# Attention's first scores among the last outputs of the feed-forward in front of it, and new orders for some first tiles

## The chip, the cores and the metric

The kernel runs on one core of one Trainium2 chip. The metric is the device time of one execution, in microseconds (us); of several runs the median counts. The engines are TensorE (PE; its weight loads, PEld, overlap its matmuls), VectorE (DVE), ScalarE (ACT), GpSimd (POOL) and SyncE (SP), which mostly issues DMAs. PE's clock is granted by a throttle; the profile shows it as a share of full speed.

## What is computed

Two layers, each with attention and a feed-forward part, and each part added to its input after a normalisation:

```python
x = L0_attn_x                                    # [2, 1024, 512] float32
x = x + _layernorm(_L0_attn_ref(_layernorm(x), Wq, bq, Wkv, bkv))
x = x + _layernorm(_L0_ffn_ref(_layernorm(x), w1, w2, w3))     # h = 1408
x = x + _layernorm(_L1_attn_ref(_layernorm(x), q_w, kv_w, c_w))
x = x + _layernorm(_L1_ffn_ref(_layernorm(x), w_gate, w_up, w_down))
```

The first attention is one within a token (32 heads of 16, four groups): no token sees another. The first feed-forward rounds its weights to −1, 0 and 1 by their mean size (`clip(round(w / mean|w|))`) and computes `sigmoid(x w1') * (x w2')`, times w3'. The second attention is causal over 1024 tokens, with 16 query heads and 4 key heads of 32, rotary positions on q and k, and a softmax of `q k' / sqrt(32)`. The second feed-forward keeps the two largest of every four hidden values. All of it is float32.

## The kernel before

The 2048 tokens are 16 tiles of 128 (x_sb, resident in SBUF). Four tiles make a group of 512 columns (GT = 4), and there are four groups (NG = 4) and two batches of eight tiles (TB = 8). One function holds everything. PE's and POOL's instructions stand in the order of the program (`manual_schedule`, L612 and L1021); those of DVE, ACT and SP are ordered by a scheduler, except for DVE in the first statistics (L613). Each engine then runs its instructions in that order, each waiting for its semaphores. Tiles come from pools, in which a tag with `bufs` buffers is used in turn, so a new tile waits for the last use of the one it replaces. Pools opened on the right side and on the left are stacks; a pool that is closed gives its room to those opened later, whose tiles wait for the uses of what lay there.

**First attention (L222 to 300).** Per tile: l0_stats (statistics, a root on ACT), l0_pre (L235: normalise on DVE, four transposes on PE into a psum bank, copy by ACT), l0_post (L243: pq and pkv, four matmuls each and one with `ones_r` and `bias` that adds the bias, L249). The bias is loaded by four small DMAs on SP's queue (L155, L156) into `braw`, behind the first four tiles of x; POOL splits it in two parts (L157 to 160: bhi, then bias). Beside it the weights of the feed-forward are loaded into large buffers (big, L129: tag raw, two buffers, used in turn by raw1, raw2, raw3 and by xTg_0 to xTg_3) and rounded: quant_sums on ACT (L312), a sum over partitions on PE (psum_w, L322) and a threshold (quant_limits, L321), quant_apply on DVE (L331).

**First feed-forward (L365 to 411, L682 to 753).** Per group g and hidden chunk hc (HC = 11): l0_hidden issues 16 ph matmuls (L371, two banks of ps_a), a sigmoid on ACT (L376), the product h on DVE (L377), and splits h into two parts hl on ACT and POOL (L379, L380). l0_out (L385) follows some chunks later (outs, L678): 8 po matmuls of a chunk into four banks. At the group's last chunk, po is normalised and added to x_sb (ln_stats with ACT's sqrt, L177; tmp on DVE, for group 3 in turn on ACT, L405; add on POOL, L411). During a group the next group's transposed input is made (l0_xT_stats, l0_xT_norm, l0_xT). In g = 2 at hc 4 the first pool p0 is closed and the pool aw opened in its room, and attention's weights are loaded there. In g = 2 at hc 5 and 9, a1_stats (L504) makes the statistics of batch 0's tiles 0 to 3 and 4 to 7; its root is made by small DVE operations (inverse_root, L182).

**Second attention, projections (project_parts, L522).** A tile's projection has three parts. First: normalise into xn (two buffers, tag xn, shared with rope's rbq and with tmp of the last norm), four transposes pxt, copy xT. Second: pq (L556) and pkv (L561), rope on DVE (ra L579, rbk and rbq L584), adds on POOL (L588). Third: transposes pkT and pqT, split into hl, two DMAs to a DRAM tile dq (L608). Batch 0's tiles 0 to 3 are projected during group 3; parts of tiles 4 to 6 stand after its last ph (L691 to 694), followed by all outputs still pending (L697, L753: four po groups, 32 matmuls).

**Second attention, tasks.** A task is a batch, a group Q of 512 queries and one key head g with its four query heads; there are 16. A task needs q (load_q, L803) and k (load_k, L809; three buffers) read back from dq on SP's queue, four DMAs each; their tiles are in pool s1, opened after the feed-forward's pools are closed (L754 to 759). score_step (L815): the product psc with the mask added by a second matmul (L824, L830), the negated maximum on DVE (mxs, L835), the exponential with its sum on ACT (L839, result thrown away in a junk tile). shifts and minus_log (L845, L873; small DVE operations) turn maxima and sums into one shift per row, which PE transposes (pmt, L795). prob_step (L893): pst (L900, L907), exponential pT (L913), for the diagonal a select on POOL (L915). value_step (L922): po (L929). Later output_parts (L939). Between them run batch 1's projections and pieces of the last feed-forward's weights (POOL, with DMAs on POOL's queue, L465). The lead-in, L1065 to 1083, is hand-written: loads of tasks 0 and 1, the remaining parts of tiles 4 to 7, the scores of task 0, then of task 1:

```python
load_upto(2)
parts[GT][2]()
...
parts[GT + 2][1]()
parts[GT + 1][2]()
...
parts[GT + 3][0]()
scores_up_to(1, -2)
parts[GT + 3][1]()
parts[GT + 2][2]()
...
```

The last feed-forward (from L1180) is not touched; its first weights are loaded when f1_begin (L1106) closes aw.

Of the kernel before, what the change touches and what calls it, by code (L numbers as in the profile page):

```python
# [24 lines left out]
def two_layer_sandwich(  # L25
# [76 lines left out]
    ones = keep.tile([P, P], F32, tag="ones", name="ones")  # L102
    nc.gpsimd.memset(ones, 1.0)
# [9 lines left out]
    aw_stack, l0_stack, p0_stack = ExitStack(), ExitStack(), ExitStack()  # L113
    p0 = p0_stack.enter_context(tc.tile_pool(name="p0", bufs=1, side="right"))
    w0 = l0_stack.enter_context(tc.tile_pool(name="w0", bufs=1))
# [12 lines left out]

    def big(name, dtype):  # L129
        return s0.tile([P, DC * H0], dtype, tag="raw", name=name)  # L130
# [23 lines left out]
    for row in (0, 32):  # L154
        nc.sync.dma_start(out=braw[row : row + 1, :D], in_=a0_bq.unsqueeze(0))  # L155
        nc.sync.dma_start(out=braw[row : row + 1, D:], in_=a0_bkv.unsqueeze(0))  # L156
# [10 lines left out]
    def ln_stats(pool, srcs, name, roots=True):  # L167

        n = len(srcs)
        st = pool.tile([P, n, 6], F32, tag=f"st{n}", name=f"st_{name}")  # L170
# [214 lines left out]
    def l0_out(g, hc, hl):  # L385
# [8 lines left out]
        if hc == HC - 1:  # L394
# [4 lines left out]
            mv, rs = ln_stats(pool, po, f"f0o_{g}")  # L399
# [104 lines left out]
    def a1_stats(st, G):  # L504
        tiles = [x_sb[:, st.b * TB + G * GT + k, :] for k in range(GT)]
        mv, rs = ln_stats(aw, tiles, f"a1_{st.b}_{G}", roots=False)
        st.ln[G] = mv, rs, minus_mean(aw, mv, rs, GT)
# [103 lines left out]

    with tc.manual_schedule(engines={mybir.EngineType.PE, mybir.EngineType.Pool}):  # L612
        with tc.manual_schedule(engines={mybir.EngineType.DVE}):  # L613
# [6 lines left out]
        th1 = quant_limits(part1, "w1", ps_o("psum_w1"))  # L620
        l0_pre(2)
        l0_post(1)
        l0_stats(1)
# [58 lines left out]
        for g in range(NG):  # L682
            nxt = None
            for hc in range(HC):
                pend.append((g, hc, l0_hidden(g, hc, xs.T)))
# [3 lines left out]
                if g == NG - 1 and hc == HC - 1:  # L689

                    parts[GT][1]()  # L691
                    parts[GT + 1][0]()
                    parts[GT + 1][1]()
                    parts[GT + 2][0]()

                if hc == HC - 1:
                    outs(2)  # L697
                elif hc != 2 and (g > 0 or hc > 2):
                    outs(1)
# [14 lines left out]
                else:  # L714
# [10 lines left out]
                    elif hc == 2 * GT + 1:  # L725
                        parts[GT - 1][2]()
                        done[0] = GT
                        parts[GT][0]()
                step = HC * g + hc
# [5 lines left out]
                if g == NG - 2 and hc == 4:  # L735
# [13 lines left out]
                    nc.sync.dma_start(out=sinq_t, in_=ropeq_sin.rearrange("(t p) f -> p t f", p=P))  # L749
                if g == NG - 2 and hc in (5, 9):  # L750
                    a1_stats(batch(0), hc // 9)
            xs = nxt
        outs(len(pend))  # L753
# [9 lines left out]
    identb = wc_pool.tile([P, P], BF16, tag="identb", name="identb")  # L763
    nc.vector.tensor_copy(identb, ident)
    cmaskb = wc_pool.tile([P, P], BF16, tag="cmaskb", name="cmaskb")
    cmask = s1.tile([P, D], F32, tag="xn", name="cmask", bufs=1)[:, :P]
    make_causal_mask(nc, cmask, mask_val=-3.0e38)
    nc.vector.tensor_copy(cmaskb, cmask)
# [31 lines left out]

    def load_q(tk):  # L803
        tk.q = s1.tile([P, REP, GW], F32, tag="q4", name=f"q4_{tk.nm}", bufs=4)
        src = tk.st.d[tk.Q][:, :, tk.g, :].rearrange("s (r d) t -> s d r t", r=REP)
        for blk in range(4):
            nc.sync.dma_start(out=tk.q[blk * DK : (blk + 1) * DK], in_=src[blk % 2])

    def load_k(st, G):  # L809
        st.k[G] = s1.tile([P, NKV, GW], F32, tag="k4", name=f"k4_{st.b}_{G}", bufs=3)  # L810
        src = st.d[G][:, :, NKV, :].rearrange("s (g d) t -> s d g t", g=NKV)
        for blk in range(4):
            nc.sync.dma_start(out=st.k[G][blk * DK : (blk + 1) * DK], in_=src[blk // 2])
# [775 lines left out]
```

## Time and profile before

| what | value |
|---|---|
| three runs | 1544.43, 1539.05, 1537.12 us |
| median | 1539.05 us |
| profiled execution | 1543.98 us |
| its span | 1542.3 us |
| granted PE clock, mean | 0.97 |
| busy: PE, DVE, ACT, POOL | 95%, 66%, 47%, 20% |
| mean DMA rate | 109 GB/s |

The profile is of one execution, and times in it are us from the start of its span. A share of busy time is a mean over stages that are bound by different things; what a change of one stage is worth is read in that stage. The chain of waits follows the work that ended last in a window back to what released it. The windows give busy times in a stretch, with the granted clock. In a timeline, brackets give an engine's idle time in front of an instruction, and what ended it.

### The profile page before, as it was taken

To read this page: it belongs to the slowest core of one execution; us is meant where nothing else is said; L and a number is where in the kernel's file an instruction comes from. 1 tells how busy PE (TensorE), PEld (TensorE's weight loads), DVE (VectorE), ACT (ScalarE), POOL (GpSimd) and SP (SyncE) were. 2 spreads that over 40 slices of the span, in tenths; PEclk is the share of its full clock that TensorE was granted. 3 is DMA by queue.
4 is the path that set the end of the run, shared out by engine and by line. 5 is a ranking of instruction groups with operands and counts; after the bars stand their busy time and mean duration, and the time that the engine had idled before them with its cause. 6 is when DMAs were issued, how large, how long until landed. Compare 5 with 4: busy or idle time off the path is not lost.

```text
span 1542.3 us, 20375 instructions
## 1 busy us (share of the span) xinstructions
PE 1466.8 (95%) x6998; PEld 1052.4 (68%) x6998; DVE 1012.8 (66%) x2408; ACT 728.6 (47%) x1849; POOL 315.8 (20%) x420
## 2 busy tenths in 40 slices
PE   7999999899779999999899999999999999999997
PEld 3558888777445544544444446888888888888886
DVE  6976456542567777656768645786578468846783
ACT  4243343232268765797686983451245034404430
POOL 1105475232302323322332002000100010001001
PEclk9999999999869999999889999999999999999998
DMA  7201211201563343243342002643353345235411
GB/s 293 75 14 41 69 55 49 48 18 52 114 159 94 94 122 98 92 133 95 96 110 109 2 1 89 246 144 143 130 210 118 143 171 191 96 143 201 161 48 75
DMA packets 78751, 167.52 MB, mean 109 GB/s; under 512 B 10100, under 2 KB 35702, under 8 KB 76600
## 3 DMA queue, kind: packets, MB, share of 16 engines
q1 hardware_dynamic: 72936, 148.40, 29.9%
q0 software_dynamic: 4656, 16.52, 2.9%
q10 hardware_dynamic: 1056, 1.31, 0.3%
q8 instruction: 55, 0.90, 0.2%
q14 instruction: 48, 0.39, 0.1%
HBM read 138.94 MB, written 27.26 MB: 108 GB/s over the span
## 4 chain that ended last, share of the span: by engine, by line
PE 75%; DVE 10%; ACT 8%; issue 3%; POOL 2%; DMA 2%; SPq 0%; ACTq 0%; DVEq 0%; POOLq 0%
PE acc L1349 12%; PE pb_u L1198 7%; PE pb_g L1198 7%; PE ph L371 7%; ACT junk L839 5%; PE po L390 4%; PE pc_g L1198 4%; PE pc_u L1198 4%; PE psc L824 4%; PE pq L248 3%; PE py L945 3%; PE pq L556 3%; PE pst L900 3%; PE po L929 3%; DVE mxs L835 3%
## 5 line engine op out<-in xcount | busy, mean ns | idle before, releaser
L835 DVE TENSOR_REDUCE mxs<-psc 128x1 f32<-128x512 f32 (+3 forms) x384 | 195.7, 551 | 83.0 <-PE psc L824 43.0
L839 ACT ACTIVATE junk<-psc,mxs 128x512 bf16<-128x512 f32 (+3 forms) x384 | 221.7, 626 | 34.1 <-DVE mxs L835 28.7
L913 ACT ACTIVATE pT<-pst 128x512 f32<-128x512 f32 (+3 forms) x384 | 159.5, 547 | 89.8 <-PE pst L907 89.4
L371 PE MATMUL ph<-xTg,w 128*128 128x512 f32 x704 | 169.9, 394 | 4.9 <-DVE h L377 2.4
L824 PE MATMUL psc<-k,q 128*128 128x512 f32 (+3 forms) x384 | 146.2, 456 | 15.6 <-ACT junk L839 8.0
L371 PEld LDWEIGHTS ph<-xTg,w 128*128 128x128 f32 x704 | 131.5, 188 | 33.6 <-DVE h L377 3.3
L900 PE MATMUL pst<-q,k 128*128 128x512 f32 (+3 forms) x384 | 123.4, 413 | 16.2 <-ACT junk L839 12.0
L824 PEld LDWEIGHTS psc<-k,q 128*128 128x128 f32 x384 | 77.9, 215 | 79.8 <-ACT pT L913 30.0
L1402 POOL TENSOR_TENSOR x_sb<-x_sb,o 128x512 f32<-128x512 f32 x14 | 19.1, 1362 | 549.2 <-DVE o L199 549.1
L1349 PE MATMUL acc<-wd,h 128*128 128x256 f32 x512 | 121.6, 379 | 0.0
L900 PEld LDWEIGHTS pst<-q,k 128*128 128x128 f32 x384 | 68.3, 197 | 61.6 <-ACT junk L839 35.1
L915 POOL TENSOR_SCALAR_AFFINE_SELECT pT<-pT 128x256 f32<-128x256 f32 x128 | 51.9, 413 | 271.2 <-ACT pT L913 268.8
L1349 PEld LDWEIGHTS acc<-wd,h 128*128 128x128 f32 x512 | 97.2, 190 | 12.9
L839 ACT ACTIVATION_READ_ACCUMULATOR junk<-psc,mxs 128x1 f32 x384 | 96.1, 251 | 0.0
L929 PE MATMUL po<-pT,v 128*32 128x512 f32 (+3 forms) x768 | 94.1, 529 | 1.3 <-POOL pT L915 0.9
L1349 PE MATMUL acc<-wd,hx 128*128 128x256 f32 x384 | 93.3, 379 | 0.0
L380 POOL TENSOR_TENSOR hl<-h,hl 128x512 fp32r<-128x512 f32 x44 | 56.9, 1297 | 162.4 <-ACT hl L379 162.3
L390 PE MATMUL po<-w,hl 128*128 128x512 f32 x352 | 87.7, 394 | 0.6 <-DVE tmp L199 0.6
L377 DVE TENSOR_TENSOR h<-h,ph 128x512 f32<-128x512 f32 x44 | 30.0, 683 | 88.3 <-PE ph L371 78.5
L1349 PEld LDWEIGHTS acc<-wd,hx 128*128 128x128 f32 x384 | 73.1, 190 | 9.8
L1259 DVE TENSOR_TENSOR gate<-gate,ab 128x1024 f32<-128x1024 f32 x32 | 39.2, 1225 | 58.9 <-ACT ab L1256 58.9
L390 PEld LDWEIGHTS po<-w,hl 128*128 128x128 f32 x352 | 66.8, 190 | 15.3 <-DVE tmp L199 1.4
(268 smaller groups left out, 2825.6 us busy)
## 6 DMA issues: line engine op xcount, KB each, us to landing
w<-kept SPq DMA_DIRECT2D x64, 512.0 KB, 5.7
q<-dq SPq DMA_DIRECT2D x64, 256.0 KB, 5.2
wd<-keptd SPq DMA_DIRECT2D x16, 1024.0 KB, 7.9
w<-in_f_wg SPq DMA_DIRECT2D x32, 384.0 KB, 3.4
w<-in_f_wu SPq DMA_DIRECT2D x32, 384.0 KB, 5.4
wd<-in_f_wd SPq DMA_DIRECT2D x16, 768.0 KB, 5.8
dq<-hl SPq DMA_DIRECT2D x32, 320.0 KB, 3.2
kept<-wl POOLq DMA_DIRECT2D x16, 512.0 KB, 3.0
```

The costliest lines, as they stand in the source:

```text
L371: nc.tensor.matmul(pa, wt[:, c, cols], xT[:, s, c, :], start=(c == 0 and s == 0), stop=(c == DC - 1 and s == 1),)
L380: nc.gpsimd.tensor_tensor(hl[:, 1, :], h, hl[:, 0, :].bitcast(F32), ALU.subtract)
L390: nc.tensor.matmul(pos0[g][k], hl[:, s, k * P : (k + 1) * P], w3[:, hc, :], start=(hc == 0 and s == 0), stop=(hc == HC - 1 and s == 1),)
L824: nc.tensor.matmul(pa[:, :w], tk.q.bitcast(F32R)[:, r, ii * P : (ii + 1) * P], st.k[ch].bitcast(F32R)[:, g, :w], start=True, stop=True,)
L835: nc.vector.tensor_reduce(mx, pa[:, :w], AX.X, ALU.max, negate=True)
L839: nc.scalar.activation(junk[:, :w], pa[:, :w], AF.Exp, bias=mx, accum_out=tk.sm[:, ii, r, ch : ch + 1])
L900: nc.tensor.matmul(pas[r][:, c0:], st.k[j // GT].bitcast(F32R)[:, g, (j % GT) * P : (j % GT + 1) * P], tk.q.bitcast(F32R)[:, r, c0:], star ...
L913: nc.scalar.activation(p[:, e, c0:], pas[2 * pr + e][:, c0:], AF.Exp)
L915: nc.gpsimd.affine_select(out=p[:, :, c0 : c0 + P], in_=p[:, :, c0 : c0 + P], compare_op=ALU.is_ge, fill=0.0, base=0, pattern=[[0, 2], [1, ...
L929: nc.tensor.matmul(tk.po[DK * r : DK * r + DK, c0:], st.v[j // GT][:, j % GT, g * DK : (g + 1) * DK], tk.pT[j, r // 2][:, r % 2, c0:], sta ...
L1198: nc.tensor.matmul(p, a[:, c, :], b[:, c, :], start=(first and c == 0), stop=(c == 1), skip_group_check=not first,)
L1349: nc.tensor.matmul(acc[m // 2][:, m % 2 * HW : (m % 2 + 1) * HW], a[:, j, k * P : (k + 1) * P], b[:, j, :], start=start, stop=True, skip_g ...
```

## The change

It has these parts.

- The four bias loads are issued on POOL's queue in place of SP's. ACT is put in program order too in the first statistics. l0_pre(2) and l0_post(1) come ahead of the first threshold (th1).
- big takes its buffers in turn from s0 (one buffer) and from a new pool rb (one buffer), which is closed in f1_begin. An eighth large tile, "qk", reuses the buffer of xTg_2; at g = 3, hc = 9, behind the third part of tile 3, task 0's k and q are loaded into it.
- Task 0's 16 scores stand after the last ph, in halves of two heads between the po groups of the last chunks, the second part of tiles 4 and 5 and the first of tiles 5 and 6. Their psum banks are from ps_a, their junk tiles from s0 (tag h).
- The last norm of the feed-forward takes its root on DVE (inverse_root) in place of ACT's sqrt.
- In g = 2 from hc = 4 on, DVE is in program order. identb and the mask are made there. a1_stats of batch 1's first half is called at g = 3, hc = 4; that of its second half takes a tile that the logarithms also use (lgp).
- k4 has two buffers. The small tiles of minus_log have one shape (small_tile). In the lead-in task 0's shifts come first, and task 1's scores stand, one step each, between parts of tiles 4 to 7. From the first pmt on, PE's order is that of before.

Cut to its core:

```diff
 def big(name, dtype):
-    return s0.tile([P, DC * H0], dtype, tag="raw", name=name)
+    n_big[0] += 1
+    if n_big[0] % 2:
+        return s0.tile([P, DC * H0], dtype, tag="raw", name=name, bufs=1)
+    return rb.tile([P, DC * H0], dtype, tag="raw", name=name)
...
 for row in (0, 32):
-    nc.sync.dma_start(out=braw[row : row + 1, :D], in_=a0_bq.unsqueeze(0))
-    nc.sync.dma_start(out=braw[row : row + 1, D:], in_=a0_bkv.unsqueeze(0))
+    nc.gpsimd.dma_start(out=braw[row : row + 1, :D], in_=a0_bq.unsqueeze(0))
+    nc.gpsimd.dma_start(out=braw[row : row + 1, D:], in_=a0_bkv.unsqueeze(0))
...
-            mv, rs = ln_stats(pool, po, f"f0o_{g}")
+            mv, rs = ln_stats(pool, po, f"f0o_{g}", roots=not last)
...
 def a1_stats(st, G):
+    late = st.b == B - 1 and G == NQ - 1
+    mv, rs = ln_stats(
+        aw, tiles, f"a1_{st.b}_{G}", roots=False, st=small_tile("lgp", "st_late") if late else None
+    )
...
-    with tc.manual_schedule(engines={mybir.EngineType.DVE}):
+    with tc.manual_schedule(engines={mybir.EngineType.DVE, mybir.EngineType.Activation}):
...
-    th1 = quant_limits(part1, "w1", ps_o("psum_w1"))
     l0_pre(2)
     l0_post(1)
+    th1 = quant_limits(part1, "w1", ps_o("psum_w1"))
...
 for hc in range(HC):
+    order = ExitStack()
+    if g == NG - 2 and hc > 3:
+        order.enter_context(tc.manual_schedule(engines={mybir.EngineType.DVE}))
...
     if g == NG - 1 and hc == HC - 1:
-        parts[GT][1]()
-        parts[GT + 1][0]()
-        parts[GT + 1][1]()
-        parts[GT + 2][0]()
+        tk = tasks[0]
+        score_sums(tk, aw)
+        halves = [
+            lambda ii=ii, r=r: score_step(
+                tk, tk.q, tk.st.k[0], ii, 0, range(r, r + 2), ps_a, waste0
+            )
+            for ii in range(GT) for r in (0, 2)
+        ]
+        out1 = lambda: outs(min(1, len(pend)))
+        for f, n in (
+            (parts[GT][1], 0), (out1, 1), (parts[GT + 1][0], 1), (out1, 1),
+            (parts[GT + 1][1], 2), (out1, 1), (parts[GT + 2][0], 1), (out1, 1),
+        ):
+            f()
+            for h in halves[:n]:
+                h()
+            del halves[:n]
...
     elif hc == 2 * GT + 1:
         parts[GT - 1][2]()
         done[0] = GT
         parts[GT][0]()
+        tk = tasks[0]
+        tk.st = batch(0)
+        both = big("qk", F32)[:, : 2 * NKV * GW].rearrange(
+            "p (n r t) -> p n r t", n=2, r=REP
+        )
+        tk.st.k[0], tk.q = both[:, 0], both[:, 1]
+        fill_k(tk.st.k[0], tk.st, 0)
+        fill_q(tk.q, tk)
...
+    if g == NG - 1 and hc == 4:
+        a1_stats(batch(1), 0)
...
-        outs(len(pend))
...
 load_upto(2)
+scored(tasks[0])
 parts[GT][2]()
 finish(0, GT)
 parts[GT + 2][1]()
 parts[GT + 1][2]()
 finish(0, GT + 1)
 bank[0] = ring
+scores_up_to(pos + 1, -1)
 parts[GT + 3][0]()
-scores_up_to(1, -2)
+scores_up_to(pos + 1, -1)
 parts[GT + 3][1]()
+scores_up_to(pos + 1, -1)
 parts[GT + 2][2]()
 finish(0, GT + 2)
-scores_up_to(2, -2)
+scores_up_to(pos + 1, -1)
 parts[GT + 3][2]()
 finish(0, GT + 3)
-scores_up_to(s_end[0], -2)
 scores_up_to(wanted(-1), -1)
```

fill_k and fill_q issue the DMAs of load_k and load_q; score_step takes the q and k tiles, the maker of banks and the maker of junk tiles as arguments; scored(task) calls shifts and puts maxima_T on the list of what is due.

## The prediction

> **What bounds the kernel now.** I read the page's slices first, for the places where TensorE (PE) is not full; then the windows and the chain of waits over each place; then the timelines of the engines that the chain names. On the page each character is one fortieth of the span (38.6 us); the first row is PE's busy share, the second the clock it was granted.
>
> ```profile
> PE   7999999899779999999899999999999999999997
> ...
> PEclk9999999999869999999889999999999999999998
> ```
>
> PE is busy 95% of the span, so time can be won only where it falls under 9: the first slice, slice 8 (from 270 us) and slices 11 and 12 (385 to 463 us), where the clock falls too. The change touches all of these and nothing else that is long.
>
> The start, in the chain of waits and the PE timeline:
>
> ```profile
> 9.69 5.96 DMA braw<-in_a_bkv
> ...
> 15.80 0.72 POOL bhi L158
> ...
> 16.60 1.53 POOL bias L159
> ```
> ```profile
> 18.94 0.50 PE L249 MATMUL pq<-bias,ones_r 64*128 64x512 f32 x1 [2.37 <-POOL bias L160]
> ```
>
> The bracket is idle time in front of the instruction and who ended it: PE stood 2.37 us for POOL, which stood for the last of four bias loads, issued behind x on SyncE (SP).
>
> The third group of the feed-forward, in the PE timeline and then VectorE's (DVE):
>
> ```profile
> 277.92 0.66 PE L212 MATMUL pt_f<-ident,xnf 128*128 128x128 f32 x4 [1.28 <-DVE h L377]
> 279.07 2.11 PE L371 MATMUL ph<-xTg,w 128*128 128x512 f32 x8 [0.49 <-ACT h L376]
> 283.53 2.75 PE L371 MATMUL ph<-xTg,w 128*128 128x512 f32 x8 [2.36 <-DVE h L377]
> ```
> ```profile
> 282.71 0.16 DVE L206 SCALAR_TENSOR_TENSOR nb<-mv_a,rs_a 128x4 f32<-128x4 f32 x1
> 282.79 0.69 DVE L377 TENSOR_TENSOR h<-h,ph 128x512 f32<-128x512 f32 x1
> ```
>
> The scheduler put both of attention's statistics (a1_stats, 268.84 to 282.8 us on DVE) ahead of the product h that frees PE's psum banks. PE waits 4.13 us, and the window 285 to 290 has a granted clock of 0.68.
>
> Feed-forward to attention, in the chain of waits and the windows (length, PE, PEld, DVE, ACT, POOL busy, clock, DMA share, GB/s):
>
> ```profile
> 396.82 7.30 PE po L390 x32
> ...
> 406.98 0.46 SPq L807
> ...
> 407.97 11.56 DMA q<-dq
> 419.53 1.28 issue
> 420.82 0.44 PE psc L824
> ...
> 422.43 4.69 PE pq L556 x8
> ```
> ```profile
> 410.00:415.00 5.00, 0.37 (x4) 0.13 (x2) 3.07 (x10) 1.23 (x3) 5.00 (x5) 0.95 1.07 213
> 415.00:420.00 5.00, 1.11 (x4) 0.71 (x4) 4.86 (x20) 2.36 (x3) 1.28 (x2) 0.50 1.08 217
> ...
> 435.00:440.00 5.00, 3.40 (x11) 1.81 (x10) 2.92 (x5) 3.23 (x11) 0.00 (x0) 0.50 0.69 184
> ```
>
> After the last po, q and k are only then loaded: their tiles overlay feed-forward buffers. PE does 1.5 us of work in 10, the clock halves, and the scores of tasks 0 and 1 then go at the pace of max (L835) and exp (L839), at half clock, to the first pmt (L795, 454.84 us) and pst (L900, 455.05 us).
>
> **Part 1, start.** The bias loads go to POOL's queue, idle from 2.30 us. POOL's other issues (L465) take 0.57 to 0.69 us: four end by 5.1 us. POOL's rows land after 3 us, SP's bias load after 5.96: 8 to 11 us. Then bhi 0.72, bias 1.53, copy 0.71 and gaps: 11.2 to 14.2 us, before pq ends at 16.57. PE's 2.37 us go, and psum_w1, moved behind the second tile, no longer waits its 0.25. The threshold comes 1.6 us later on DVE, which has idle gaps of 1 to 1.9 us per tile here, and w1 is first needed at 112 us. Late next: nothing on PE. If loads from POOL land after 13.4 us the gain shrinks to nothing. **−2.5 (−3 to 0).**
>
> **Part 2, third group.** DVE follows the program: h of chunks 6 and 7 no longer stands behind a1_stats. At chunk 5 DVE has h, 0.67, and a1_stats: four statistics of 0.6, four of 0.1, some 14 small dependent operations 0.2 apart, 5.6 us. With h that is a period of PE (16 ph 3.69 and 8 po 1.82: 5.5 us) plus 0.8, so h(6) may be 1 us late, against 2.36 and 1.28 now. Won: 4.13 idle and 5 × 0.32 = 1.6 of clock, less about 0.7. The mask, made here now, is a few tenths on POOL and DVE. In-order DVE may also stand for an ACT copy at the transposes. **−5 (−6 to −3).** a1_stats of batch 1's first half goes into group 4, where PE is full and DVE has room: 0.
>
> **Part 3, the transition.** Times are those of before. ph of the last chunk ends 384.06; pq and pkv of tile 4 (3.60 + 1.73) and one po group (1.82) bring PE to the first score at 391.05. Its data: the write of tile 3 is issued on SP at 380.74 and lands 3.2 (the page's row) to 4 us later, at 384 to 385; only then eight loads of 256 KB run, 2 MB at the 208 to 221 GB/s of these loads now, 9.7 us, and 1.5 to start and finish. T0, the first score, is at about 396.5, and PE **waits 5.4 us where it did not wait before**. This is a new wait of an in-order queue: behind it stand po of the last three chunks, pq of tile 5, and so the last norm, x of tile 7 and every other projection. The 10 us hole at 410 goes in exchange.
>
> From T0 PE has 16 scores with mask (0.2, 0.24, 0.31, 0.43 wide by wide: 4.7), three po groups 5.5, pq and pkv of tile 5 (5.2), two transposes 0.9: 16.3, plus 2 for some 4 us at half clock: last po at T0+18.5. k and q transposes of tile 4 to T0+20; pq of tile 6 waits for a bank held by task 0's last exps, 2 us, and runs 5.2: T0+27.3; transposes of tile 5, T0+28. Beside it DVE has the last norm: four statistics 2.6, 14 small operations where ACT's sqrt (with two table loads of 1.28) was, mixed with task 0's logarithm: T0+26.6. Then four tmp and POOL adds (1.25 each) through two buffers that rope shares: T0+32.6, xn and transposes of tile 7 T0+33.9, copy 0.6, its pq and pkv at a clock lowered by the 6 us hole (4.69 + 1.74 was such a pair): T0+41.5; rope 1.9, POOL 1.25, transposes: T0+45.5; task 1's remaining scores lie beside that. First pst at about 442.5 to 443 against 455.05: **−12.**
>
> Bounds. Were PE alone the limit, with 34 us from T0 (the 16.3, another 16 scores 4.7, two pq and pkv 10.4, four pairs of transposes 2.2, one pxt 0.4), pst would come at 430.5, 24.5 earlier, less 2.5 for the clock: −22. If task 1's q, queued on SP behind wc (last po) and the write of tile 5, or the POOL chain is 7 us later than I have it: −5. I take −12, nearest to the rows of the chain.
>
> The trace has the clock at 0.95 as PE falls idle at 410 and at 0.50 from 415 to 420. The Trainium skill ("TensorE: Matmul & The Clock Gate", Part 1) says that one idle window of about 3.4 us halves the clock and about 3.4 us of work restores it, and its "Why this matters for your kernels" warns of gaps over 3 us: this speaks against the change's new wait. By the page, an estimate, the wait would cost 1.7 us more. The trace had 0.50 from 435 to 450 too, with PE two thirds busy, and that row is what the clock's 2 us after T0 and rival (c) rest on.
>
> **Part 4, later.** a1_stats of batch 1's second half, 5.6 us of DVE, lay in the hole and now shares a buffer with the logarithms in running attention, where DVE and ACT set the pace in turn. All hidden 0, none 5.6; attention has DVE at 6 to 8 tenths: **+1.5 (0 to 3).** One k buffer fewer: batch 1's last k replaces one used until task 7 in both versions: 0.
>
> **Sum.** −2.5 − 5 − 12 + 1.5 = −18. The profiled run took 1543.98 us (span 1542.3), so 1526 for it; it lay 4.9 above the median of the three runs, 1539.05, from which the forecast is **1521**. All bounds: −31 to −5, that is 1508 to 1534.
>
> **Rivals.** (a) The wait is moved, not removed: T0's wait and the POOL chain eat the transition (−5 or less), a1_stats costs 3. −2.5 − 5 − 3 + 3 is about −7: 1532. For it: the same write, load, max and exp chain is still there. Against: 7.3 us of po and a pair of projections now lie beside it.
> (b) PE-bound lead-in: −2.5 − 5.5 − 22 + 0.5, about −30: 1509. For it: the hole at 410 is the only place where PE had no work in its queue. Against: tile 7 needs the last po, and its chain over DVE, POOL and ACT is 15 us with only 7 of PE work beside it.
> (c) Slower, by the clock: the new wait at 391 and the hole near T0+30 hold the lead-in at half clock. Of the 46 us from T0, 34 are PE work at full clock and 12 waits: it ends at 396.5 + 12 + 34/c. At c = 0.5 that is 476.5, 21 late, and −7.5 + 1.5 leaves +15: 1554. It decides from c = 0.65 (no gain in all), and shows as over 0.5% slower below c = 0.57. For it: the trace has 0.50 for 15 us on end in this stage. Against: from T0 PE has 16 us without a pause, and before it was at 1.00 again in 425 to 430, after 5 us of work.
>
> **Chances.** Forecast (gains of 10 to 25) 0.62; (a) 0.17, of which 0.11 within half a per cent; (b) 0.11; (c) 0.10, of which 0.07 over half a per cent. This kernel's measurement tells about 0.5% (7.7 us) from no change: faster 0.62 + 0.11 + 0.06 = 0.79, same 0.14, slower 0.07. Range 1508 to 1535: it leaves out (c) and what of (a) gains under 4 us, some 0.15.
>
> **What would show it.** Start: the bracket before pq<-bias gone. Group 3: no DVE h bracket above 1 us between 270 and 290. Transition: a bracket of 4 to 7 us before the first psc, by q<-dq; first pst some 12 us plus 7.5 earlier than 455 (435 to 437 on its own axis); pxt of tile 7 waiting on x_sb (L411) or xn; no table load there. I am wrong if q lands much later than 14 us after tile 3's write is issued, if the clock stays near 0.5 after the first score, or if attention from then on has new DVE waits.

## The result, and the profile after

Fourteen runs of the changed kernel have a median of 1542.9 us (1537.4 to 1548.08), fourteen of the kernel before 1542.27 (1537.12 to 1549.41; the three shown ahead of the prediction are among them). The ratio is 1.0005, 95% interval 0.9986 to 1.0024: no change that can be told, where I forecast 1521 (from three runs of before; −18 from the 1542.27 of fourteen would be 1524). The profiled execution took 1541.6 us (span 1539.8), that of before 1543.98 (1542.3): in the two traces the change is worth 2.43 us of span.

The two rows of the page's slices that were shown of before:

```profile
PE   7999999999788898999899999999999999999997
...
PEclk9999999999899899999899999999999999999998
```

The dip at slice 8 is gone. Of the two at 385 to 463 us, slice 11 still has 7, and slice 12 has 8 in place of 7 and 9 tenths of the clock in place of 6. But slices 13 and 14 (463 to 539 us) and slice 16 have fallen from 9 to 8, and with slice 14 the clock; nothing in my sum lay there but Part 4's 1.5 us. The traces, cut at instructions that both have (the start of the span, the first ph matmul of a chunk, the first pst of a task):

| stretch | before, us | after, us | change | forecast | at half clock, before and after, us |
|---|---|---|---|---|---|
| start to ph of g = 0, hc = 4 | 128.32 | 131.81 | +3.49 | −2.5 | 0, 6.8 |
| g = 0, hc = 4 to g = 3, hc = 10 (the third group is in it) | 251.97 | 248.02 | −3.95 | −5 | 3.4, 0 |
| transition, from there to pst of task 0 | 74.76 | 65.31 | −9.45 | −12 | 27.3, 17.1 |
| task 0 to 1 | 17.23 | 20.71 | +3.48 | 0 | 6.8, 0 |
| task 1 to 3 | 49.66 | 49.51 | −0.15 | 0 | 6.8, 10.2 |
| task 3 to 4 | 23.94 | 30.29 | +6.35 | +1.5 | 0, 10.2 |
| task 4 to the end | 996.40 | 994.19 | −2.21 | 0 | 49.1, 39.2 |

The transition's 9.45 us are given back in full by the first pst of task 4 (+9.68), and the start gives back the third group. Of the 15.6 us of span by which the −18 was missed, 8.2 lie between the first pst of task 0 and that of task 4, 6.0 in the start, 2.5 in the transition and 1.1 before it; behind task 4, 2.2 us came back.

**Start.** POOL's timeline of after, then PE's, then DVE's:

```profile
9.66 0.72 POOL L167 CAST bhi<-braw 64x640 fp32r<-64x640 f32 x1 [5.19 <-DMA braw<-in_a_bkv]
```
```profile
17.24 0.50 PE L259 MATMUL pq<-bias,ones_r 64*128 64x512 f32 x1
...
73.28 0.66 PE L222 MATMUL pt_a<-ident,xna 128*128 128x128 f32 x4 [1.66 <-DVE xna L209]
```
```profile
66.78 3.82 DVE L209 TENSOR_SCALAR ao<-ao,mv_ao,rs_ao 128x512 f32<-128x512 f32 x4
...
72.52 0.71 DVE L209 TENSOR_SCALAR xna<-x_sb,mv_a,rs_a 128x512 f32<-128x512 f32 x1
```

The bias is split from 9.66 us on in place of 15.80, the bracket before pq<-bias is gone, and PE is 2.0 us ahead of before up to tile 10's transposes (65.77 against 67.80 us). Then DVE, in program order, does four normalisations of tile 0's group (3.82 us) ahead of tile 11's input: PE stands 1.66 us and the clock falls to half for 3.4 us at 74 us. It falls again at 115, where gaps of 0.73 and 0.94 us stand (0.73 and 0.75 before, without a fall).

**Third group.** Of the three brackets shown of before, one is left, with another releaser:

```profile
281.66 1.10 PE L222 MATMUL pt_f<-ident,xnf 128*128 128x128 f32 x8 [1.52 <-ACT hl L389]
```

The stretch also has a cost that the sum did not have. Within a chunk, ph matmuls of before start 227 ns apart (the median) in all four groups. In after it is 234 ns in groups 0 and 2, and 227 in groups 1 and 3, and the same holds in all ten kernels of the experiments that were made from after; e3 and e8, made from before, have 227 throughout. Groups 0 and 2 are those whose xTg lies in the new pool rb. An estimate: 352 matmuls at 7 ns more, 2.5 us, of which 0.4 lie in the start's stretch. That the place in memory is the cause is not shown, since no run has the new pool alone.

**Transition.** The chain of waits of after, then PE's timeline:

```profile
386.91 8.59 DMA qk<-dq
```
```profile
395.84 0.45 PE L665 MATMUL psc<-qk 128*128 128x128 f32 x1 [5.09 <-DMA qk<-dq]
...
429.77 0.44 PE L665 MATMUL psc<-qk,q 128*128 128x128 f32 x1 [3.43 <-DVE rbk L598]
```

and its windows, with the columns as before (the clock is the third number from the end):

```profile
390.00:395.00 5.00, 0.75 (x4) 0.29 (x2) 0.00 (x0) 0.00 (x0) 1.65 (x2) 0.97 0.94 185
395.00:400.00 5.00, 3.38 (x14) 3.04 (x15) 1.17 (x4) 3.16 (x10) 0.00 (x0) 0.50 0.00 0
400.00:405.00 5.00, 5.00 (x13) 3.25 (x12) 0.85 (x2) 1.46 (x7) 0.00 (x0) 0.51 0.02 5
```

The new wait is there, 5.09 us in front of the first psc at 395.84 (T0; forecast 396.5 in the time of before, so 396.0 on this axis). The clock is at half for 10.2 us behind it, although PE is full from 400 us. The second wait, 3.43 us for rope on DVE, is the hole near T0+30 that the prediction had; 6.8 us at half clock lie at it.

**The running attention.** Two new waits of PE, in its timeline, each for a bank that an exponential (junk) frees, which waits for a maximum (mxs) on DVE:

```profile
465.15 0.38 PE L665 MATMUL psc<-qk,q 128*128 128x256 f32 x1 [2.87 <-ACT junk L678]
...
531.47 0.48 PE L665 MATMUL psc<-k,q 128*128 128x128 f32 x1 [2.60 <-ACT junk L678]
```

Why the maxima were late, in DVE's timeline of after:

```profile
460.72 0.18 DVE L924 TENSOR_SCALAR lge<-sms 128x16 int32<-128x16 int32 x1 [1.14 <-ACT junk L678]
...
464.16 0.23 DVE L889 TENSOR_TENSOR pm<-r,pm 128x16 bf16<-128x16 f32 x1
464.26 2.20 DVE L676 TENSOR_REDUCE mxs<-psc 128x1 f32<-128x128 f32 x8
...
521.42 0.69 DVE L184 BATCH_NORM_STATS2 st_late<-x_sb 128x6 f32<-128x512 f32 x1
...
529.93 3.26 DVE L676 TENSOR_REDUCE mxs<-psc 128x1 f32<-128x512 f32 x8
```

and the same two places in that of before, where the scheduler had put maxima between the steps of the logarithm, and where DVE waited for PE ahead of task 5's maxima:

```profile
471.33 0.33 DVE L862 SCALAR_TENSOR_TENSOR lgz<-lgf,lgz 128x16 f32<-128x16 f32 x1
471.58 0.28 DVE L835 TENSOR_REDUCE mxs<-psc 128x1 f32<-128x128 f32 x1
471.78 0.16 DVE L863 TENSOR_TENSOR lgy<-lgz 128x16 f32<-128x16 f32 x1
...
532.95 1.29 DVE L835 TENSOR_REDUCE mxs<-psc 128x1 f32<-128x512 f32 x2 [1.57 <-PE psc L824]
```

In after the eighteen operations of task 2's logarithm stand in one block of 3.6 us with eight maxima behind it. From 521 us on the late statistics (st_late, Part 4), six of the small operations of their root and, between them, a tile's rope put off task 5's maxima to 529.93; the clock falls to half for 10.2 us.

### The profile page after: what moved, and what is told of

It is laid out like the page before. It is cut to its first block, busy times and chain, and to the rows that moved or that the text cites. A ratio compares the mean times of both kernels' runs of the same rounds, so it can differ in the third digit from the quotient of the medians.

```text
span 1539.8 us, 20389 instructions
## 1 busy us (share of the span) xinstructions
PE 1468.4 (95%) x6998; PEld 1052.8 (68%) x6998; DVE 1019.3 (66%) x2420; ACT 727.3 (47%) x1847; POOL 319.2 (21%) x424
## 4 chain that ended last, share of the span: by engine, by line
PE 78%; DVE 10%; ACT 7%; issue 2%; DMA 1%; POOL 1%; SPq 0%; ACTq 0%; DVEq 0%; POOLq 0%
PE acc L1419 13%; PE ph L381 9%; PE pb_u L1268 7%; PE pb_g L1268 7%; ACT junk L678 4%; PE po L400 4%; PE psc L665 4%; PE pq L258 4%; PE pc_u L1268 4%; PE pc_g L1268 4%; PE py L1015 4%; PE pst L970 3%; PE po L999 3%; PE pq L570 3%; DVE mxs L676 3%; ACT pT L983 2%
## 5 line engine op out<-in xcount | busy, mean ns | idle before, releaser
L678 ACT ACTIVATE junk<-psc,mxs 128x512 bf16<-128x512 f32 (+3 forms) x384 | 222.2, 631 | 32.3 <-DVE mxs L676 28.2
L1419 PEld LDWEIGHTS acc<-wd,h 128*128 128x128 f32 x512 | 97.0, 190 | 13.1
L665 PE MATMUL psc<-k,q 128*128 128x512 f32 (+3 forms) x256 | 92.3, 429 | 6.4 <-ACT junk L678 5.3
L970 PE MATMUL pst<-q,k 128*128 128x512 f32 (+3 forms) x256 | 80.0, 405 | 14.7 <-ACT junk L678 9.7
L665 PEld LDWEIGHTS psc<-k,q 128*128 128x128 f32 x256 | 49.4, 202 | 46.9 <-ACT pT L983 20.9
L1329 DVE TENSOR_TENSOR gate<-gate,ab 128x1024 f32<-128x1024 f32 x32 | 39.2, 1225 | 59.2 <-ACT ab L1326 59.2
L970 PEld LDWEIGHTS pst<-q,k 128*128 128x128 f32 x256 | 45.0, 197 | 47.7 <-ACT junk L678 23.9
```

The costliest lines, as they stand in the source:

```text
L665: nc.tensor.matmul(pa[:, :w], q.bitcast(F32R)[:, r, ii * P : (ii + 1) * P], k.bitcast(F32R)[:, g, :w], start=True, stop=True,)
L678: nc.scalar.activation(junk[:, :w], pa[:, :w], AF.Exp, bias=mx, accum_out=tk.sm[:, ii, r, ch : ch + 1])
L970: nc.tensor.matmul(pas[r][:, c0:], st.k[j // GT].bitcast(F32R)[:, g, (j % GT) * P : (j % GT + 1) * P], tk.q.bitcast(F32R)[:, r, c0:], star ...
L1419: nc.tensor.matmul(acc[m // 2][:, m % 2 * HW : (m % 2 + 1) * HW], a[:, j, k * P : (k + 1) * P], b[:, j, :], start=start, stop=True, skip_g ...
```

## The experiments

The theory: every gain is real where I put it, and it is given back on DVE, by the late statistics (task 3 to 4), by the logarithm in one block (task 0 to 1) and by the order at the start. The rival: attention's first tasks, or the clock, bring PE back to the same time whatever is taken out of DVE. Each ratio is against the kernel before in runs on the same chip. Stretches are those of the profiled executions; "total" is the median of the runs. The runs were taken in sets, and before itself has medians of 1540.46 to 1542.86 in them, so totals of different sets compare to some 2 us; the ratios are the safer measure.

| kernel | start to hc 4 | to g = 3, hc 10 | transition | task 0 to 4 | rest | total | ratio, 95% interval |
|---|---|---|---|---|---|---|---|
| before | 128.32 | 251.97 | 74.76 | 90.83 | 996.40 | 1542.27 | |
| after | 131.81 | 248.02 | 65.31 | 100.52 | 994.19 | 1542.90 | 1.0005 (0.9986–1.0024) |
| e1, statistics early | 127.21 | 247.95 | 70.20 | 98.68 | 993.42 | 1541.46 | 1.0007 (0.9989–1.0025) |
| e2, start undone | 132.88 | 248.13 | 63.22 | 104.73 | 991.82 | 1543.52 | 1.0013 (0.9995–1.0031) |
| e3, third group alone | 128.02 | 246.31 | 74.24 | 91.36 | 992.10 | 1536.12 | 0.9961 (0.9944–0.9978) |
| e4, scores later | 131.01 | 247.97 | 58.07 | 105.53 | 994.39 | 1538.53 | 0.9978 (0.9960–0.9996) |
| e5, logarithm behind | 129.97 | 247.96 | 64.80 | 101.63 | 996.33 | 1540.97 | 0.9990 (0.9974–1.0005) |
| e6, e4 + e5 + e11 | 130.54 | 247.96 | 59.26 | 94.99 | 996.67 | 1531.39 | 0.9933 (0.9908–0.9959) |
| e7, e6 with old start | 129.17 | 248.01 | 60.02 | 96.15 | 996.21 | 1530.91 | 0.9924 (0.9901–0.9947) |
| e8, e3 with bias on POOL | 128.63 | 246.19 | 74.99 | 90.87 | 992.09 | 1537.05 | 0.9976 (0.9957–0.9996) |
| e9, logarithms in pairs | 132.48 | 247.02 | 58.41 | 103.39 | 995.26 | 1539.93 | 0.9982 (0.9966–0.9998) |
| e10, e9 with new start, add later | 129.06 | 248.00 | 59.73 | 104.88 | 993.79 | 1535.72 | 0.9959 (0.9943–0.9974) |
| e11, statistics in the hole | 130.42 | 247.98 | 65.51 | 97.69 | 998.62 | 1535.75 | 0.9953 (0.9930–0.9975) |
| e12, all together | 128.98 | 248.04 | 59.44 | 95.34 | 993.75 | 1526.89 | 0.9906 (0.9887–0.9925) |

**e1.** After, with the late statistics given their own tile and left to the scheduler:

```diff
-    late = st.b == B - 1 and G == NQ - 1
+    late = False
```

> The changed kernel, but the statistics of batch 1's second half take a tile of their own, so that the scheduler may put them anywhere again. Theory A (the late statistics stand on DVE ahead of task 5's maxima and cost PE 2.6 and 0.8 us of waits and a stretch at half clock): from the first pst of task 3 to that of task 4 it takes about 24 us as in the kernel before (23.9), not 30.3; the statistics cost 0 to 3 us in the lead-in instead; the time falls by 3 to 6 us against the changed kernel. Theory B (running attention is held by something else, so that an earlier start is absorbed by task 4 whatever is done): task 4's first pst stays within 1.5 us of 545.7 and the time does not move.

Task 3 to 4 falls from 30.29 to 24.13 us, so the statistics are that cost. The total does not move: the scheduler now puts them ahead of task 1's first maxima, and the transition grows by 4.9. What follows: the term is found, but where they go decides whether it is saved.

**e2.** After, with the start of before:

```diff
-nc.gpsimd.dma_start(out=braw[row : row + 1, :D], in_=a0_bq.unsqueeze(0))
+nc.sync.dma_start(out=braw[row : row + 1, :D], in_=a0_bq.unsqueeze(0))
...
-with tc.manual_schedule(engines={mybir.EngineType.DVE, mybir.EngineType.Activation}):
+with tc.manual_schedule(engines={mybir.EngineType.DVE}):
...
+th1 = quant_limits(part1, "w1", ps_o("psum_w1"))
 l0_pre(2)
 l0_post(1)
-th1 = quant_limits(part1, "w1", ps_o("psum_w1"))
```

> The changed kernel with the first stage as in the kernel before: bias loads on SP's queue, threshold ahead of the second tile, ACT left to the scheduler in the first statistics. Theory A (the bias wait's 2 us are won, but the order that DVE then gets puts four ao operations ahead of tile 11's normalisation and costs more): PE's 2.4 us bracket is back, no bracket before pt_a of tile 11, ph of chunk 4 of the first group at about 128.3 as in the kernel before against 131.8, and the whole is 1.5 to 3.5 us faster than the changed kernel. Theory B (the start is a gain, and the later loss a chance of the clock): ph of chunk 4 at 130 or later, the whole slower by 0 to 2 us.

The bracket before pq<-bias is back (2.31 us) and psum_w has one of 1.72, but the bracket at tile 11 is gone; the stretch is 132.88 us, 1.07 longer than in after and 4.56 longer than the same code in before. With the old start it is 128.02 to 132.88 in four profiles (before, e2, e3, e9), with the new one 127.21 to 131.81 in six (after, e1, e4, e5, e6, e11). The start's worth lies inside this scatter, in which stretches at half clock have a large part: 6.8 us in e2, none in before, 6.8 in after, none in e1.

**e3.** Before, with only Part 2's core:

```diff
 for hc in range(HC):
+    order = ExitStack()
+    if g == NG - 2 and hc > 3:
+        order.enter_context(tc.manual_schedule(engines={mybir.EngineType.DVE}))
...
+    order.close()
```

> The kernel before with one part of the change: DVE in program order in the third group from chunk 4 on. Theory A (the gain of this stage is real and stays): DVE h brackets of 1.28 and 2.36 us gone, ph of chunk 9 at 284 to 285.5 against 289.7, everything behind it earlier by 4 to 5 us, the time 4 to 5 us lower. Theory B (it is absorbed by the transition or by attention): ph of chunk 9 earlier, but the first pst of task 0 or of task 4 at its old time, the time unchanged.

The only bracket left in the group, in PE's timeline of e3:

```profile
276.52 1.09 PE L212 MATMUL pt_f<-ident,xnf 128*128 128x128 f32 x8 [0.98 <-ACT hl L379]
```

The stretch falls by 5.66 us and the pst of task 4 comes 5.95 earlier (539.93): nothing is given back. The total is 0.39% less (0.22 to 0.56%), or 4.5 us by the two medians of its set. One order of DVE, in seven chunks, does more than the whole change.

**e4.** After, with task 0's scores behind the projection of tile 5, so that PE does not stand for q:

```diff
-(parts[GT][1], 0), (out1, 1), (parts[GT + 1][0], 1), (out1, 1),
-(parts[GT + 1][1], 2), (out1, 1), (parts[GT + 2][0], 1), (out1, 1),
+(parts[GT][1], 0), (out1, 0), (parts[GT + 1][0], 0), (out1, 0),
+(parts[GT + 1][1], 2), (out1, 2), (parts[GT + 2][0], 2), (out1, 2),
```

> The changed kernel with task 0's scores behind the po groups of chunks 8 and 9's places and tile 5's pq: po and pq of tile 5 fill the wait for q. Theory A (PE's wait at the first score, 4 to 5 us, is on the path): the bracket before the first psc is gone or under 1 us, tile 7's pxt and the first pst of task 0 come 2 to 5 us earlier than in the changed kernel (431.3 and 445.1). Theory B (the path runs over task 0's maxima and exponentials on DVE and ACT, which start from the same q): the first pst comes at the same time or up to 3 us later.

The first bracket of the scores, in PE's timeline:

```profile
398.36 0.30 PE L665 MATMUL psc<-qk 128*128 128x128 f32 x1 [0.53 <-DVE rbk L598]
```

The wait for q is gone, and the transition is 58.07 us, 7.24 less: the 5.09 and what the clock had lost behind it (10.2 us at half clock in place of 17.1). First pst is at 437.05. Tasks 0 to 4 give 5.0 back, and the median is 4.4 under that of after, with intervals that overlap.

**e5.** After, with task 2's logarithm two score steps later, and DVE in program order in the first four steps of the loop, so that the maxima come first:

```diff
-scored(tk)
+waiting_logs.append(tk)
+while waiting_logs and (
+    waiting_logs[0].n not in (2, 3)
+    or pos >= min(s_end[waiting_logs[0].n] + 2, len(s_steps))
+):
+    scored(waiting_logs.pop(0))
...
+if step < 4:
+    order.enter_context(tc.manual_schedule(engines={mybir.EngineType.DVE}))
```

> The changed kernel, with task 2's logarithm (18 small DVE operations, 3.7 us) emitted two score steps later and DVE in program order in the first four probability steps, so that the first eight maxima of task 3 come ahead of it. Theory A (PE's 2.87 us wait before a psc at 465 and the half clock behind it come from this order): that bracket gone, from the first pst of task 0 to that of task 2 it takes 42 to 44 us against 45.9 in the changed kernel and 42.2 in the kernel before; the time falls by 2 to 5 us. Theory B (maxima and exponentials are behind anyway, and PE waits as long a little later): same 45 to 49 us, time unchanged.

PE's timeline:

```profile
466.48 0.40 PE L977 MATMUL pst<-mT,onesb 32*128 32x512 bf16 x4 [2.87 <-DVE mT L898]
```

The bracket of 2.87 us before psc is now one of 2.87 before pst, since the copy of the row of shifts (mT) stands on DVE behind the logarithm. Task 0 to 1 is 1.5 shorter, task 1 to 2 4.3 longer. That is the rival: the wait was moved, and the logarithm is 3.6 us of DVE wherever it stands in one block.

**e11.** After, with the late statistics written into the hole of the lead-in, where DVE's order is fixed:

```diff
-    late = st.b == B - 1 and G == NQ - 1
+    late = False
...
-scores_up_to(pos + 1, -1)
-parts[GT + 3][0]()
-scores_up_to(pos + 1, -1)
-parts[GT + 3][1]()
+with tc.manual_schedule(engines={mybir.EngineType.DVE}):
+    scores_up_to(pos + 1, -1)
+    parts[GT + 3][0]()
+    scores_up_to(pos + 1, -1)
+    a1_stats(batch(1), NQ - 1)
+    parts[GT + 3][1]()
```

> The changed kernel with one edit: the statistics of batch 1's second half stand between task 1's second score step and tile 7's rope. Theory A (late statistics cost PE some 6 us between task 3 and task 4 and fit into DVE's idle time in the lead-in): first pst of task 3 to that of task 4 23.6 to 24.2 us against 30.3, the transition 0 to 2 us longer than 65.3, the time 3 to 6 us under the changed kernel. Theory B (the place does not matter): the transition is as much longer as the later stretch is shorter, time unchanged.

DVE's timeline at the hole and at task 5's maxima:

```profile
432.21 0.68 DVE L184 BATCH_NORM_STATS2 st_a<-x_sb 128x6 f32<-128x512 f32 x1
...
528.93 1.29 DVE L676 TENSOR_REDUCE mxs<-psc 128x1 f32<-128x512 f32 x2 [1.56 <-PE psc L665]
```

At 527 DVE now waits for PE. Task 3 to 4 falls from 30.29 to 23.26 us and the transition is the same (65.51 against 65.31): the statistics cost nothing there. The median is 7.2 us under that of after. Of this the profile shows 4.06 at the first pst of task 4; its rest, 998.62, is 4.4 longer than in after, with 25.5 us at half clock between tasks 8 and 12 (15.2 in after), so this one profile, of the slowest of the ten runs, shows less than the median does.

**e6.** After with the edits of e4, e5 and e11, as shown there.

> The changed kernel with three edits at once: scores of task 0 behind tile 5's pq, task 2's logarithm behind task 3's first maxima, and the statistics of batch 1's second half between task 1's second score step and tile 7's rope, where DVE stood idle for 4.3 us. Theory A (the gain of the transition is real and is lost on DVE's order only): from ph of the last chunk to the first pst of task 0 some 58 to 61 us, on to task 4's first pst 91 to 96 us, the whole 10 to 15 us under the kernel before, 1526 to 1531. Theory B (what is won at the front is lost again up to task 4 by something else): task 4's first pst within 4 us of 545, the time within 5 us of the kernel before.

The transition is 59.26 and task 3 to 4 23.64, as with each edit alone; first pst of task 4 is 13.1 us earlier than in before, and 12.9 arrive at the end. So nothing pulls PE back to one time: the rival falls. The logarithm's 2.87 us stay, before mT.

**e7 and e8.** e7 is e6 with the edits of e2 but for its first (the bias stays on POOL); e8 is e3 with the bias on POOL:

```diff
-nc.sync.dma_start(out=braw[row : row + 1, :D], in_=a0_bq.unsqueeze(0))
+nc.gpsimd.dma_start(out=braw[row : row + 1, :D], in_=a0_bq.unsqueeze(0))
```

> As the run of all three edits, but the first stage in the order of the kernel before, with only the bias loads on POOL's queue. Theory A (the new order of the first tiles costs 1.7 us of idle time before tile 11's transposes and now and then a clock window): no bracket before pt_a of tile 11, ph of chunk 4 of the first group at 125.5 to 127, 1 to 4 us faster than the run of all three. Theory B (the order is not what costs): ph of chunk 4 as in the other runs with the new start, 127 to 131.

> The kernel before with two parts of the change: DVE in program order in the third group, and the bias loads on POOL's queue with everything else of the start as it was. Theory A (the bias wait is worth about 2.4 us once the order of the first tiles stays): PE's bracket before pq<-bias gone, ph of chunk 4 of the first group at about 126, the time 6 to 8 us under the kernel before (4.5 of it from the third group). Theory B (the wait only moves to the sums of the weights, psum_w, or to a later normalisation): 4 to 5 us under it, as with the third group alone.

PE's timeline of e8:

```profile
21.36 0.38 PE L322 MATMUL psum_w<-part_w,ones 128*128 128x4 f32 x2 [1.96 <-ACT abs_w L315]
```

The bias no longer holds PE, and the next thing does: the sum for the threshold, 1.96 us where before had 0.25. The total of e8 is that of e3, and e7's that of e6, within their intervals.

**e9, e10 and e12.** The logarithm of tasks 2 and 3 in pairs of operations between the maxima. e9 has this in place of e5's edit, beside e4's, e11's and e2's, with DVE in program order for eight steps of the loop; e10 is e9 with the new start and l0_add(0) behind l0_pre(11); e12 is e10 with program order for four steps:

```diff
+for rr in (r, r + 1):
+    score_step(tk, tk.q, tk.st.k[ch], ii, ch, range(rr, rr + 1), ring, waste)
+    some()
...
-        l0_add(0, ao)
...
         l0_pre(11)
+        l0_add(0, ao)
...
-if step < 8:
+if step < 4:
```

> All three edits, with the whole first stage as in the kernel before, and with the logarithms of tasks 2 and 3 cut into pairs of operations between their neighbours' maxima (DVE in program order in the first eight probability steps), since moved as one block the logarithm only made the shift of task 1 late: a 2.87 us wait before its pst. Theory A (DVE's order, not its load, is what holds PE between the first psts of tasks 0 and 2): that wait and the 2.87 us one before a psc both gone, 42 to 45 us from the first pst of task 0 to that of task 2 (47.5 with the block moved), and 1526 to 1530 in all. Theory B (DVE and ACT have no room there, and the wait turns up elsewhere): 46 to 49 us, 1530 to 1533.

> As the run before it, but with the changed kernel's start, in which the adds of the first four tiles (four ao normalisations on DVE, 3.8 us beside POOL) come behind tile 11's normalisation. Theory A (the new start loses by those four operations in front of tile 11's): no bracket before pt_a of tile 11, none before pq<-bias and psum_w, ph of chunk 4 of the first group at 125.5 to 127.5, 1 to 3 us faster than the run with the old start. Theory B (the loss only moves to another tile, or the clock window falls in any case): a bracket before another pt_a, ph of chunk 4 at 128 to 131.

> The changed kernel with task 0's first scores behind tile 5's q, the late first-layer normalisations put on VectorE into the hole of the lead-in, the logarithms of tasks 2 and 3 in pairs behind the maxima with VectorE's order written out for the first four steps of the loop only, and the start's in-place normalisation of tile 0 one step later. Theory A (what cost the kernel with the logarithms in pairs its gain was VectorE's written order in steps 4 to 7, which put batch 1's tiles late): first pst of task 0 to that of task 1 takes 17 to 18 us, task 1 to task 2 25 to 28, and the whole 1526 to 1530 us, ratio 0.990 to 0.9925. Theory B (the wait for task 2's logarithm only moves on to the copy of mT, whatever the order of steps 4 to 7): task 0 to task 2 takes 47 us or more as in the kernel with all three edits, and the whole stays at 1531 to 1535.

e9 gets task 0 to 1 in 17.21 us, but task 1 to 2 takes 34.44 and 2 to 3 28.42: in steps 4 to 7 program order puts batch 1's normalisations late (brackets of 1.63 and 1.94 us before pxt), and the clock is at half for 17.1 us from 481. e10 has the same there (34.37 and 28.45). In its start no bracket is left at pq<-bias, psum_w or tile 11, and ph begins at 107.71 us, 3.1 earlier than in before. But then, in its windows:

```profile
70.00:75.00 5.00, 5.00 (x17) 2.50 (x17) 5.00 (x10) 0.85 (x2) 4.14 (x3) 1.00 0.00 0
110.00:115.00 5.00, 5.00 (x13) 3.84 (x13) 0.10 (x1) 0.60 (x1) 0.00 (x0) 0.50 0.00 0
```

the clock is whole at tile 11 and at half for 6.8 us from 109, at brackets of 0.73 and 1.42 us in front of the first ph matmuls, and at hc = 4 the 3.1 are gone. e12 differs from e10 in the four steps alone: 34.37 becomes 29.03 and 28.45 becomes 23.98, 9.8 us in all, and the total falls by 8.8 (6.4 if each is set against before in its own set). That is what theory A expected, and its total (1526 to 1530) holds. Its stretches do not: task 0 to 1 took 18.67 and 1 to 2 29.03, a sum of 47.7 that is what B expected and that e6 had (47.5). PE's timeline of e12:

```profile
458.50 0.40 PE L977 MATMUL pst<-mT,onesb 32*128 32x512 bf16 x4 [1.21 <-DVE mT L898]
```

The bracket at mT fell from 2.87 to 1.21, with nothing gained in the sum. So the logarithms in pairs are not shown to be worth anything. What e12 has over e6 in the profiles lies at the start (1.56 us) and behind task 4 (2.92: from there to the last feed-forward it has 27.3 us at half clock, e6 37.5, at nearly the same idle time of PE, 22.6 and 22.2; that part is the clock's). e12 is the best version: 0.94% under before (0.75 to 1.13%), and 14 to 16 us under after: 16 by the medians as they are, 14 with each set against before in its own set.

## Why the prediction was wrong, point by point

**Part 4 is the step that failed: "+1.5 (0 to 3)".** It cost 6.35 us in the profile (4.8 in e2 and in e4, by their 28.77 and 28.78 against 23.94), outside its range; undone well (e11) it is worth 7.2 of the median, with intervals of the two ratios that do not meet. I priced 5.6 us of DVE against a mean share of 6 to 8 tenths. The mean says nothing of the place: the scheduler put the statistics straight ahead of the maxima that free PE's psum banks. The text had "none 5.6" for nothing hidden, and still closed the range at 3; it should have stood at 5.6 and something for the clock.

**"1526 for it" also took for granted that what follows the first pst keeps its length.** The 3.48 us at task 0 to 1 have no term in the sum. The text listed "new DVE waits" from then on as a way to be wrong, without a price, though of all DVE's order around the first tasks only the scheduler decides. Where scores, shifts and statistics were moved, the order of what is left had to be compared on DVE, as it was for the third group. Tasks 0 to 4 took 90.8 to 91.4 us in the three profiles with the lead-in of before (before, e3, e8), and 97.7 to 105.5 in all with the lead-in of after, except e6, e7 and e12 (95.0 to 96.2). This is the largest part of the loss: 9.7 us here against the 1.5 that the sum had.

**Part 1, "−2.5 (−3 to 0)": wrong.** The bias loads did land early (pq<-bias has no bracket), but "Late next: nothing on PE" was false: DVE's program order at tile 11 and the clock took it back. Without the bracket at tile 11 (e10) ph begins 3.1 us earlier, and the clock takes most of that too. What the start is worth by itself is not settled; the medians of e6 and e7 (1531.39, 1530.91) say nothing or little.

**Part 2, "−5 (−6 to −3)": right.** −3.95 in after over the whole stretch, −5.66 in e3, where the total is 0.39% less. The 1.7 us between the two are in part the slower ph matmuls of groups 0 and 2, for which the sum had no term, and in part a longer bracket (1.52 against 0.98).

**Part 3, "−12 (−22 to −5)": the mechanism right, the size a little off.** T0 was forecast to 0.2 us and the wait to 0.3 (5.09). The POOL chain decides tile 7, as forecast. From T0 to the first pst I had 46 to 46.5 us; it took 49.30. (One step of that sum is off by 0.6: 33.9, 0.6, 4.69 and 1.74 make 40.9, not 41.5.) Two us of the 3 can be seen in DVE's timeline of after, where two operations of task 0's logarithm stood beside POOL's four adds. They are on the chain of waits, and the rope behind them ends PE's wait of 3.43 us:

```profile
426.64 1.19 DVE L940 TENSOR_TENSOR lgw<-lgw,mxs 128x16 f32<-128x16 f32 x1
427.86 1.21 DVE L886 CAST pm<-lgw 128x16 bf16<-128x16 f32 x1
```

0.17 and 0.20 us each in the block at 463 us, so 2.0 us more here. The Trainium skill ("TensorE: Matmul & The Clock Gate", "Why this matters for your kernels") warns of gaps of PE over 3 us. The trace agrees at this wait: 0.97 in the window of the wait, 0.50 behind it. But half clock followed shorter gaps too, such as the 1.66 us at tile 11, so what the runs show is stricter. e4, which takes the wait away, cut the transition by 2.15 us more than the wait itself; by the page's window (an estimate) it would be 1.7.

**Rivals.** (a) had the right shape, the gain eaten by DVE, but put it at T0 and into tile 7's chain, where only some 2.5 us of it were. (c), by the clock, did not happen in the lead-in: 17.1 us at half clock against 27.3. The clock is a part of the loss, but behind DVE's waits: 10.2 us at half clock at 531.

**What stays open.** What the start is worth, and why the ph matmuls of two groups are slower. What the logarithm in one block costs by itself, since in e5, e6 and e12 it moved and never went; and how much of the 3 us by which profiles of e1, e2, e4 and e11 are longer than after at task 1 to 2 (28.2 to 28.4 against 25.23, at the same idle time of 1.1 to 1.2 and 12.8 to 14.7 us at half clock against 6.8) is chance of the clock and how much is theirs.

## What to carry to other kernels

Work that is moved off a hole must be priced at the instruction in front of which it lands, on each engine that a scheduler orders: compare that engine's order ahead of the next instruction that frees PE's banks, and take the whole duration as the upper bound. A gain far up in the program arrives at the end only if none of the stretches behind it has got longer, so cut both traces at common instructions and account for every stretch, not only for those that the change was meant for. Try the parts alone: here one of them was worth 4.5 to 6 us by itself, and another cost about as much. And compare the time from start to start of instructions that were not meant to change: here 7 ns on each of 352 matmuls went unseen in the sum.

## What the runs showed of the hardware

**Small DVE operations wait for POOL's adds.** In e4 four operations of the logarithm took 1.18 to 1.26 us where the same take 0.17, each beside an add of POOL. In DVE's and POOL's timelines of e4:

```profile
413.94 1.26 DVE L935 TENSOR_TENSOR lgp<-lgp,lgy 128x16 f32<-128x16 f32 x1
415.23 1.18 DVE L936 SCALAR_TENSOR_TENSOR lgp<-lgp,lgy 128x16 f32<-128x16 f32 x1
```
```profile
413.90 2.48 POOL L421 TENSOR_TENSOR x_sb<-x_sb,tmp 128x512 f32<-128x512 f32 x2 [6.45 <-DVE lgp L934]
```

POOL's two adds, 1.24 us each, begin 0.04 us ahead of the first operation and end with the second: DVE got through one per add. The Trainium skill ("SBUF — State Buffer", "Who interferes with whom") says that a DVE instruction with two SBUF inputs contends with a GpSimd instruction that reads SBUF, and that this is an exclusive lock. These rows agree: lgp<-lgp,lgy has two such inputs. The CAST pm<-lgw of after, shown above, has one, and took 1.21 us beside the adds as well.

**The clock falls in stretches of 3.4 us or multiples of it:** 3.4, 6.8, 10.2 or 17.1 us, once 20.5 (e8). Short gaps sometimes cost a stretch and sometimes not: gaps of 0.73 and 0.94 us at the first ph matmuls had one in after, and the same gaps (0.73 and 0.93) none in e1.

The traces show what differs. In each of them the falls begin whole multiples of 3.41 us apart, as on a grid, and the grid lies elsewhere in each execution. In after both gaps lie in one step of it (111.39 to 114.80 us, 1.66 us idle together), and the next step is at half clock; in e1 the grid parts them (0.60 and 1.05 us), and no fall follows. The gap at tile 11 does the same: 1.66 us in one step and a fall in after, 1.22 and 0.44 us in two steps and none in e1.

I counted the steps from 60 to 900 us in all 14 profiles, with PE's idle time in each and the clock of the next:

| step | idle time of PE in it | steps | next step at half clock |
|---|---|---|---|
| at full clock | under 0.5 us | 2751 | 2 |
| at full clock | 0.5 to under 2 us | 341 | 157 |
| at full clock | 2 us or more | 43 | 42 |
| at half clock | under 0.2 us | 233 | 34 |
| at half clock | 0.2 us or more | 77 | 75 |

So half a microsecond of idle time in a step can be enough, and the way back asks for a step that is almost full. The clock of after, at half until 404.9 us though PE was full from 400 us, fits this: the step from 398.11 on still had 0.53 us of idle time. Where a gap will fall on the grid is not known beforehand, so its price is known beforehand only as a mean over runs, and a stretch of one profile can be 3 us longer than the same instructions in another.
